# A graph layer's two small matrix products, on halves of the TensorE array and on all of it

## The chip, the cores and the metric

One core of a Trainium2 chip runs the kernel; the other cores are idle. The metric is the device time of one execution in microseconds (us). Two measurements of this kernel agree within about 0.2%.

## The reference

A message-passing layer on 12,500 nodes and 400,000 edges, then a residual and a layer norm. An edge takes the features of its source node, multiplies them with weights that a small network makes of the edge's 64 scalars, and with the edge's four attributes (one scalar `e0`, one vector `e1`); the results are summed by destination node. The edges come sorted by destination. Cut to what matters:

```python
h_s, h_v = (s @ lin1_ws) * a, (v @ lin1_wv) * a          # per node, scaled
hid = silu(edge_scalars @ fc_w1 * _inv(64))               # per edge, 64 wide
w = hid @ fc_w2 * _inv(64)                                # per edge, 224 wide
w1, w2, w3, w4, w5 = split(w, [64, 128, 160, 192])
es, ev = h_s[edge_src], h_v[edge_src]                     # gather
m_s1 = w1 * es * e0
m_s2 = w4 * einsum('eci,ei->ec', ev, e1) * _inv(3)
m_v1 = (w2 * es)[:, :, None] * e1[:, None, :]
m_v2 = w3[:, :, None] * ev * e0[:, :, None]
m_v3 = w5[:, :, None] * cross(ev, e1[:, None, :]) * _inv(2)
agg_s = segment_sum(concat(m_s1, m_s2), edge_dst) / 4
agg_v = segment_sum(concat(m_v1, m_v2, m_v3), edge_dst) / 4
# lin2 on the sums, self-connection, gates, then
x = layernorm(x + concat(silu(scalars), gated))
```

All of it is in fp32.

## The kernel before

**Nodes first.** A stage ahead of the loop computes the node features (`hp`, L283, and `pz`, L298), scales them on DVE and writes them to a table in HBM, `h_tab`.

**Edges in tiles, blocks and steps.** 128 edges are a tile (3125 of them). Three tiles are a block (`BT`), whose edges' destinations lie in a window of 16 nodes (`W`). Blocks go in pairs: an even block is half 0, an odd one half 1. A step of the main loop (L744) handles a quad of four tiles, two of each half; there are 782 steps, the last with one tile. What a step does:

- POOL gathers the source rows, one indirect DMA for each tile, 128 rows of `h_tab` into `hg` (L433). Four `hg` buffers stand in turn, and POOL runs ahead as far as they allow.
- Every second step `hide` makes the hidden layer of two steps ahead: `ph` (L424) multiplies the block-diagonal `w1` (64 + 64 rows) with 128 rows of edge scalars, in which the two halves lie one above the other. ACT applies the silu into `hid` (L426), so the hidden values of half 0 stand in partitions 0 to 63 and those of half 1 in 64 to 127.
- `weights` (L445) makes the 224 weights of each edge: for each tile a product with 64 rows of `hid` as the stationary side and `w2` as the moving side, into one of two `pw` buffers of PSUM. `w2` holds `fc_w2` twice, once for each half of the rows.
- `products` (L455, L463) on DVE multiplies weights and gathered features into `pr`, 416 columns for each tile. `select_quad` (L501, L504) makes the selection on DVE: `oh` says which of the block's 16 nodes an edge goes to, `sel` is that times the four edge attributes, 64 columns for each tile.
- `sum_up`, one step later, adds a tile's edges up on TensorE: `add_tile` (L511) multiplies the tile's `sel` (128 edges by 64) with its `pr` (128 by 416) into `pa`. Half 0 writes the PSUM partitions 0 to 63 and half 1 the partitions 64 to 127, so that a pair of blocks shares one `pa`.
- When both blocks of a pair are summed, ACT copies `pa` to `sa` (L676); two steps later four transposes, `pt` (L520), turn it round. After 16 blocks, `po` (L536) applies the output map: two sums of five 128-row products, one of which has a further one on 32 rows of `t3`, named `po<-t` in the profile. DVE adds the 16 windows into the node sums `acc` at addresses that it reads from `rows` (L544, L720), two in a step.
- Between these, `finish` (L547) closes four tiles of nodes at a time: transposes `pp` (L570) into `z`, gates, residual, moments, norm; and the self-connection `psc` (L656) is added in pieces.

**Order.** The loop's instructions stand on PE, DVE, ACT and POOL in the order of the code (`manual_schedule`). On PE a step is: pw of step n, pp if a job is being turned, the sums of step n-1, ph for step n+2 (every second step), po and pt when due, psc when due. On DVE: the first product, z, reads of window addresses, the other products, `oh`, `sel`, two adds, one step of a closing job. The misc tiles in PSUM (ph, pt, po, pp, psc) share two buffers. SP issues the loads.

**Shapes.** A product on 64 rows, or into 64 columns, uses half of the array, as `128*64` and `64*128` tell in the profile. Every product is fp32 and shows as two weight loads (PEld) and two matmul passes (PE).

After the loop there is a repair path (L807 to L854), which runs only when a block's window is wider than 16 nodes or the schedule's margin is broken. It did not run in this execution.

Of the kernel before, what the change touches and what calls it, by code (L numbers as in the profile page):

```python
# [10 lines left out]
F32 = mybir.dt.float32  # L11
# [9 lines left out]
P = 128  # L21
S = 64
# [6 lines left out]
BT = 3  # L29
EB = BT * P  # L30
W = 16
Q = 4
# [7 lines left out]
NWT = 224  # L40
NPR = 2 * S + 3 * V3
ROWS = 4 * W
# [10 lines left out]
def gnn_kernel(  # L53
# [21 lines left out]
    nc = tc.nc  # L75
# [5 lines left out]
    TT = G * GT  # L81
# [6 lines left out]
    consts = ctx.enter_context(tc.tile_pool(name="consts", bufs=1))  # L88
# [15 lines left out]
    for i in range(2):  # L104
        r = slice(S + i * V, S + (i + 1) * V)
# [126 lines left out]
    w1 = consts.tile([2 * S, 2 * S], F32, name="w1")  # L232
    nc.vector.memset(w1, 0.0)

    w2 = consts.tile([2 * S, NWT], F32, name="w2")
    l2 = consts.tile([P, 11, V3], F32, name="l2")
    nc.vector.memset(l2, 0.0)
    share = ends_pool.tile([1, NB], I32, name="share")
# [6 lines left out]
    with tc.tile_pool(name="nodes", bufs=2) as nodes, tc.tile_pool(  # L245
        name="nodes_ps", bufs=6, space=PSUM
    ) as nps, tc.tile_pool(name="z_ps", bufs=2, space=PSUM) as zps:
        CH = 4 * U * P
        HALF = CH // 2
        for c0 in range(0, N, CH):  # L250
            cn = min(CH, N - c0)
            quarters = 4 if cn == CH else 1
            assert quarters == 4 or cn <= U * P
            xas = []
            for b0 in range(0, cn, HALF):
                bn = min(HALF, cn - b0)
                xa = nodes.tile([P, HALF], F32, name="xa", bufs=3)
                nc.sync.dma_start(xa[:S, :bn], xs_t[:, c0 + b0:c0 + b0 + bn])
                nc.sync.dma_start(xa[S:, :bn], xv_t[:2 * V, c0 + b0:c0 + b0 + bn])
                xas.append(xa)  # L260
            xz = nodes.tile([P, U * P], F32, name="xz")
            cq = cn // quarters
            for q in range(quarters):
                nc.sync.dma_start(xz[q * V:(q + 1) * V, :cq],
                                  xv_t[2 * V:, c0 + q * cq:c0 + (q + 1) * cq])
            if c0 == 2 * CH:
                for half in range(2):
                    r = slice(half * S, (half + 1) * S)
                    nc.sync.dma_start(w1[r, r], fc_w1)
                    at_c = 0  # L270
                    for a, b in ((64, 128), (0, 64), (192, 224), (160, 192), (128, 160)):
                        nc.sync.dma_start(w2[r, at_c:at_c + b - a], fc_w2[:, a:b])
                        at_c += b - a
            ht = nodes.tile([P, 4 * U, D], F32, name="ht")
            nt = -(-cn // P)
            first = c0 // P
            full = cn // P
            for t0 in range(0, nt, U):
                ps = nps.tile([P, U, P], F32, name="hp")
                for t in range(t0, min(t0 + U, nt)):  # L280
                    n = min(P, cn - t * P)
                    e = t * P % HALF
                    nc.tensor.matmul(ps[:n, t - t0], xas[t * P // HALF][:, e:e + n], l1,  # L283
                                     start=True, stop=True)
                k = min(U, full - t0)
                nc.vector.tensor_mul(
                    ht[:, t0:t0 + k, :P], ps[:, :k],
                    at[:, first + t0:first + t0 + k, None].to_broadcast([P, k, P]))
                if t0 + k < nt <= t0 + U:
                    n = cn - full * P  # L290
                    nc.vector.tensor_scalar(ht[:n, full, :P], ps[:n, full - t0],
                                            at[:n, first + full:first + full + 1], None, op0=OP.mult)

            pz = zps.tile([P, U, 4, V], F32, name="pz")
            k = quarters * V
            for u in range(-(-cq // P)):
                n = min(P, cq - u * P)
                nc.tensor.matmul(pz[:n, u, :quarters].rearrange("p q c -> p (q c)"),  # L298
                                 xz[:k, u * P:u * P + n], l1z[:k, :k], start=True, stop=True)
            if quarters == 4:  # L300
                nc.vector.tensor_mul(
                    ht[:, :, P:].rearrange("p (q u) c -> p u q c", q=4), pz,
                    at[:, first:first + 4 * U].rearrange("p (q u) -> p u q", q=4)[:, :, :, None]
                    .to_broadcast([P, U, 4, V]))
            else:
                nc.vector.tensor_mul(ht[:, :full, P:], pz[:, :full, 0],
                                     at[:, first:first + full, None].to_broadcast([P, full, V]))
            if cn > full * P:
                n = cn - full * P
                nc.vector.tensor_scalar(ht[:n, full, P:], pz[:n, full, 0],  # L310
                                        at[:n, first + full:first + full + 1], None, op0=OP.mult)
            nc.scalar.dma_start(
                h_tab[c0:c0 + full * P, :].rearrange("(q p) d -> p q d", p=P), ht[:, :full])
            if cn > full * P:
                nc.scalar.dma_start(h_tab[c0 + full * P:c0 + cn, :], ht[:n, full])
# [99 lines left out]
    def hidden(pool, psum, es, halves, t0, n):  # L415

        ph = psum.tile([2 * S, Q * P], F32, name="ph", tag="misc")
        hid = pool.tile([2 * S, Q * P], F32, name="hid")
        ends = [max(0, min(n, m - t0)) for m in halves]
        assert ends[0] >= ends[1]  # L420
        for k, c0, c1 in ((2 * S, 0, ends[1]), (S, ends[1], ends[0])):
            if c1 > c0:
                c = slice(c0 * P, c1 * P)
                nc.tensor.matmul(ph[:k, c], w1[:k, :k], es[:k, t0 * P + c0 * P:t0 * P + c1 * P],  # L424
                                 start=True, stop=True)
                nc.scalar.activation(hid[:k, c], ph[:k, c], AF.Silu, scale=1.0 / math.sqrt(64))  # L426
        return hid
# [10 lines left out]
    def weights(psum, hid, slots):  # L438

        pw = psum.tile([P, Q, 256], F32, name="pw")  # L440
        n = len(slots)
        for t in sorted(range(n), key=lambda t: (slots[t][1], slots[t][0])):
            half, c = slots[t]
            r = slice(half * S, (half + 1) * S)
            nc.tensor.matmul(pw[:, t, :NWT], hid[r, c * P:(c + 1) * P], w2[r],  # L445
                             start=True, stop=True)
        return pw

# [46 lines left out]
    def select_quad(pool, tiles):  # L495

        n = len(tiles)
        t0 = slot_of[tiles[0][0]]
        u = t0 % AHEAD
        oh = pool.tile([P, Q, W], F32, name="oh4")[:, :n]  # L500
        nc.vector.tensor_tensor(oh, rel[:, t0:t0 + n, None].to_broadcast([P, n, W]),  # L501
                                iota[:, None, :].to_broadcast([P, n, W]), op=OP.is_equal)
        sel = pool.tile([P, Q, 4, W], F32, name="sel")
        nc.vector.tensor_mul(  # L504
            sel[:, :n], oh[:, :, None, :].to_broadcast([P, n, 4, W]),
            by_slot(tiles[0][0])[:, u:u + n, :, None].to_broadcast([P, n, 4, W]))
        return sel

    def add_tile(pa, half, sel, t, pr, start, stop):

        nc.tensor.matmul(pa[half * ROWS:(half + 1) * ROWS, :NPR],  # L511
                         sel[:, t].rearrange("p k w -> p (k w)"), pr, start=start, stop=stop)

    def turned(psum, sa, tt, t3, b, n):

# [98 lines left out]
    with tc.tile_pool(  # L614
# [47 lines left out]
        pas = {}  # L662
# [11 lines left out]
        def close(j, n):  # L674
            sa = late.tile([P, NPR], F32, name="sa")
            nc.scalar.copy(sa, pas.pop(j)[:, :NPR])  # L676
            turns_due.append((n + 2, j, sa))
# [22 lines left out]
        def sum_up(n, tiles, pr, sel):  # L700

            for slot, (t, half, _) in sorted(enumerate(tiles), key=lambda k: (k[1][2], k[1][1])):
                b, m = divmod(t, BT)
                j = b // 2
                assert b % 2 == half
                if j not in pas and m == 0:
                    pas[j] = pa_ps.tile([P, 512], F32, name="pa")
                stop = m == BT - 1 or t == TT - 1
                add_tile(pas[j], half, sel, slot, pr[:, slot], start=(m == 0), stop=stop)
                if stop:  # L710
                    ended.add(b)
                    if {2 * j, 2 * j + 1} <= ended:
                        close(j, n)

        def add_up(n):

# [91 lines left out]
        with tc.For_i(0, n_redo, 1):  # L808
# [5 lines left out]
            with tc.For_i(0, n_again, 1) as g, tc.For_i(0, GT, 1) as k:  # L814
# [21 lines left out]
                with tc.For_i(first + W, last + 1, W) as base:  # L836
# [1 line left out]
                        base, 0, N - 1, skip_runtime_bounds_check_because="it is at most `last`")  # L838
                    pa = pa_ps.tile([P, 512], F32, name="pa")
                    sel = select(late, r, eat)  # L840
                    add_tile(pa, 0, sel, 0, pr[:, 0], start=True, stop=True)
                    sa = late.tile([P, NPR], F32, name="sa")
                    nc.scalar.copy(sa[:ROWS], pa[:ROWS, :NPR])
                    tt = late.tile([P, 7, NO, W], F32, name="tt", bufs=1)
# [56 lines left out]
```

## Time and profile before

| What | Value |
|---|---|
| Time, median of 10 runs | 4089.33 us (4087.28 to 4093.45) |
| The profiled execution: time | 4091.91 us |
| The profiled execution: span | 4090.0 us |
| Mean granted TensorE clock | 0.929 |
| Start of the first pw, second sum, last sum | 92.21, 134.34, 4055.78 us |
| HBM traffic, mean | 100 GB/s |

The profile gives an instruction's line, engine, operation and the tiles that it writes and reads (`pa<-pr,sel`), its partitions and elements, its count, busy time and mean duration, and the idle time of its engine ahead of it with what ended it. For PE, `128*64 128x416` is a stationary side of 128 rows and 64 columns, and 416 columns that stream through it. "Busy" is the union of an engine's instructions in time, so overlapping passes count once. The granted clock is the share of full speed that TensorE was given; in this profile it is either 1 or one half at any moment.

### The profile page before, as it was taken

Reading aid. Unit: us, or ns where it says so; the run is one execution under the profiler, and the core shown is the slowest. Engines: PE = TensorE matmul, PEld = TensorE weight load, DVE = VectorE, ACT = ScalarE, POOL = GpSimd, SP = SyncE. Lnnn points to the kernel's source line nnn. Section 1 sums busy time; section 2 is a strip of 40 time slices with the busy share of each in tenths; the row PEclk is TensorE's granted clock in tenths of the full one; section 3 lists DMA queues with packets and bytes.
Section 4 is the critical chain, followed back from the end, with each engine's and each line's share of the span. In section 5 each row is a group of like instructions: output and inputs, shape, how many; then the busy total and the mean of one; then the engine's idle time right before and its main releaser. Section 6 shows DMA issues by size and latency. Waiting matters only on the chain.

```text
span 4090.0 us, 56919 instructions
## 1 busy us (share of the span) xinstructions
PE 3312.5 (81%) x17386; PEld 1601.3 (39%) x17386; DVE 2527.5 (62%) x6359; ACT 932.2 (23%) x3007; POOL 3010.8 (74%) x3134
## 2 busy tenths in 40 slices
PE   4678888888887888887888888788888788788886
PEld 4334433433443443343343343343334334334333
DVE  2665665666666666666656666666666666666665
ACT  0111221222222222222222122122222222222221
POOL 3677777777777777777777777777777777777774
PEclk7899999999999998999999999999999999999998
DMA  7434443443443443434434334344343443443431
GB/s 207 109 92 100 102 104 95 101 101 97 101 101 98 104 98 98 108 94 101 102 97 106 95 100 106 94 101 102 98 109 90 100 110 90 104 105 90 105 93 48
DMA packets 292610, 414.51 MB, mean 101 GB/s; under 512 B 74869, under 2 KB 239618, under 8 KB 292053
## 3 DMA queue, kind: packets, MB, share of 16 engines
q0 software_dynamic: 150000, 256.20, 24.1%
q1 hardware_dynamic: 128770, 145.95, 15.6%
q10 hardware_dynamic: 13526, 8.64, 0.7%
q8 instruction: 141, 2.31, 0.2%
q14 instruction: 173, 1.41, 0.1%
HBM read 394.54 MB, written 16.01 MB: 100 GB/s over the span
## 4 chain that ended last, share of the span: by engine, by line
POOL 28%; issue 22%; DMA 19%; DVE 14%; PE 13%; DVEq 3%; ACTq 0%; ACT 0%; POOLq 0%; SPq 0%
POOL hg L433 28%; DMA hg<-h_tab,idx 18%; DVE pr L463 8%; PE pa L511 5%; DVE pr L455 2%; PE ph L424 2%; PE pw L445 2%; DVEq L720 2%; PE po L536 2%; DVE acc L544 1%; PE pt L520 1%; DVE sel L504 1%; DVE oh L501 1%; DMA h_tab<-ht 1%; PE hp L283 0%
## 5 line engine op out<-in xcount | busy, mean ns | idle before, releaser
L433 POOL DMA_INDIRECT hg<-h_tab,idx x3125 | 2988.1, 956 | 1036.9 <-issue 905.7
L511 PE MATMUL pa<-pr,sel 128*64 128x416 f32 x6250 | 1372.0, 562 | 631.3 <-DVE acc L544 324.4
L455 DVE TENSOR_TENSOR pr<-pw,hg 128x512 f32<-128x512 f32 x782 | 540.3, 691 | 1325.5 <-DMA hg<-h_tab,idx 1011.6
L463 DVE TENSOR_TENSOR pr<-pw,hg 128x384 f32<-128x384 f32 x2346 | 1205.6, 552 | 90.2 <-issue 22.4
L511 PEld LDWEIGHTS pa<-pr,sel 128*64 128x64 f32 x6250 | 411.2, 143 | 1212.0 <-issue 746.7
L445 PE MATMUL pw<-w,hid 64*128 64x224 f32 x6250 | 821.9, 377 | 17.1 <-ACT hid L426 17.1
L445 PEld LDWEIGHTS pw<-w,hid 64*128 64x128 f32 x6250 | 544.0, 187 | 319.5 <-issue 301.1
L676 ACT COPY sa<-pa 128x416 f32<-128x416 f32 x521 | 263.1, 505 | 1170.7 <-PE pa L511 1170.5
L424 PE MATMUL ph<-es,w 128*128 128x512 f32 (+1 forms) x784 | 490.2, 710 | 1.9 <-DMA es<-in_es_t_dram 1.3
L426 ACT ACTIVATE hid<-ph 128x512 f32<-128x512 f32 x392 | 233.5, 596 | 973.7 <-PE ph L424 973.2
L520 PEld LDWEIGHTS pt<-ident,sa 128*128 128x128 f32 (+1 forms) x2084 | 225.7, 135 | 343.1 <-issue 235.6
L504 DVE TENSOR_TENSOR sel<-oh,eas 128x256 f32<-128x256 f32 x782 | 333.6, 427 | 37.1
L520 PE MATMUL pt<-ident,sa 128*128 128x128 f32 (+1 forms) x2084 | 336.4, 285 | 4.9 <-DVE z L571 4.9
L536 PE MATMUL po<-tt,l 128*96 128x256 f32 (+3 forms) x1340 | 317.3, 384 | 3.1 <-ACT t L527 3.1
L524 ACT COPY tt<-pt 128x192 f32<-128x192 f32 x521 | 164.8, 316 | 475.5 <-PE pt L520 471.4
L536 PEld LDWEIGHTS po<-tt,l 128*96 128x96 f32 x1340 | 206.6, 164 | 126.3 <-issue 64.4
L424 PEld LDWEIGHTS ph<-es,w 128*128 128x128 f32 x784 | 130.9, 210 | 303.9 <-issue 277.9
L544 DVE TENSOR_TENSOR acc<-acc,os 96x32 f32 x1042 | 194.3, 186 | 30.2 <-DVE acc L544 8.9
L501 DVE TENSOR_TENSOR oh<-rel,iota 128x64 f32<-128x64 int16 x782 | 174.7, 223 | 0.0
L539 ACT COPY os<-po 96x512 f32<-96x512 f32 (+2 forms) x67 | 38.2, 570 | 314.8 <-PE po L536 296.4
L526 ACT COPY tt<-pt 128x32 f32<-128x32 f32 x521 | 102.9, 198 | 0.0
L426 ACT ACT_TABLE_LOAD x47 | 60.3, 1283 | 173.6 <-PE ph L424 91.3
(70 smaller groups left out, 748.9 us busy)
## 6 DMA issues: line engine op xcount, KB each, us to landing
es<-in_es_t_dram SPq DMA_DIRECT2D x260, 384.0 KB
hg<-h_tab,idx POOLq DMA_INDIRECT x3125
h_tab<-ht ACTq DMA_DIRECT2D x6, 1280.0 KB
xt<-in_x_dram SPq DMA_DIRECT2D x23, 320.0 KB
out_dram<-y SPq DMA_DIRECT2D x23, 320.0 KB
xv<-in_xv_t_dram SPq DMA_DIRECT2D x25, 187.5 KB
eat<-in_ea_dram SPq DMA_DIRECT2D x30, 120.0 KB
xs<-in_xs_t_dram SPq DMA_DIRECT2D x25, 125.0 KB
```

The source lines that it names most:

```text
L424: nc.tensor.matmul(ph[:k, c], w1[:k, :k], es[:k, t0 * P + c0 * P:t0 * P + c1 * P], start=True, stop=True)
L426: nc.scalar.activation(hid[:k, c], ph[:k, c], AF.Silu, scale=1.0 / math.sqrt(64))
L433: nc.gpsimd.indirect_dma_start(out=hg[:, t, :], out_offset=None, in_=h_tab, in_offset=bass.IndirectOffsetOnAxis(ap=i, axis=0))
L445: nc.tensor.matmul(pw[:, t, :NWT], hid[r, c * P:(c + 1) * P], w2[r], start=True, stop=True)
L455: nc.vector.tensor_mul(two, pw[:, :n, :2 * S].rearrange("p t (k c) -> p t k c", k=2), hg[:, :n, None, :S].to_broadcast([P, n, 2, S]))
L463: nc.vector.tensor_mul(pr[:, :n, first:first + V3].rearrange("p t (i c) -> p t i c", i=3), pw[:, :n, None, 2 * S + k * V:2 * S + (k + 1) * ...
L504: nc.vector.tensor_mul(sel[:, :n], oh[:, :, None, :].to_broadcast([P, n, 4, W]), by_slot(tiles[0][0])[:, u:u + n, :, None].to_broadcast([P ...
L511: nc.tensor.matmul(pa[half * ROWS:(half + 1) * ROWS, :NPR], sel[:, t].rearrange("p k w -> p (k w)"), pr, start=start, stop=stop)
L520: nc.tensor.transpose(pt[:c, four * P:four * P + k], sa[:k, four * P:four * P + c], ident[:k, :k])
L536: nc.tensor.matmul(po[:, k, :nb], l2[:b, terms[to, part, four]], a[:, :nb], start=(n == 0), stop=(n == len(of) - 1))
L544: nc.vector.tensor_add(window, window, os[:, :, b])
L676: nc.scalar.copy(sa, pas.pop(j)[:, :NPR])
```

## The change

**Weights.** `w2` becomes two maps, one for each half: rows 0 to 63 of map 0 and rows 64 to 127 of map 1 hold `fc_w2`, the other rows are zero. The product takes all 128 rows of `hid`, both halves' hidden values, and the zero rows take the wrong half out.

**Sums.** The selection has 128 columns for each tile, 64 for half 0 and 64 for half 1; the columns of the other half are zero. They are zeroed once, in two buffers that the steps use in turn. The selection's multiplication on DVE is done for each half. The product then writes all 128 partitions of `pa`, and a pair's six products are one accumulation, begun by the first tile of half 0 and ended by whichever tile comes last.

The number of products is the same: 3125 for the weights and 3125 for the sums.

```diff
-    w2 = consts.tile([2 * S, NWT], F32, name="w2")
+    w2 = consts.tile([2 * S, 2, NWT], F32, name="w2")
+    nc.vector.memset(w2, 0.0)
...
-                        nc.sync.dma_start(w2[r, at_c:at_c + b - a], fc_w2[:, a:b])
+                        nc.sync.dma_start(w2[r, half, at_c:at_c + b - a], fc_w2[:, a:b])
...
+                if k < 2 * S:
+                    nc.vector.memset(hid[k:, c], 0.0)
...
-            r = slice(half * S, (half + 1) * S)
-            nc.tensor.matmul(pw[:, t, :NWT], hid[r, c * P:(c + 1) * P], w2[r],
+            nc.tensor.matmul(pw[:, t, :NWT], hid[:, c * P:(c + 1) * P], w2[:, half],
                              start=True, stop=True)
...
-        sel = pool.tile([P, Q, 4, W], F32, name="sel")
-        nc.vector.tensor_mul(
-            sel[:, :n], oh[:, :, None, :].to_broadcast([P, n, 4, W]),
-            by_slot(tiles[0][0])[:, u:u + n, :, None].to_broadcast([P, n, 4, W]))
+        sel = sels[t0 // Q % len(sels)]
+        eas = by_slot(tiles[0][0])
+        for half in range(2):
+            k = slice(2 * half, min(2 * half + 2, n))
+            m = k.stop - k.start
+            if m > 0:
+                assert all(h == half for _, h, _ in tiles[k])
+                nc.vector.tensor_mul(
+                    sel[:, k, half], oh[:, k, None, :].to_broadcast([P, m, 4, W]),
+                    eas[:, u + k.start:u + k.stop, :, None].to_broadcast([P, m, 4, W]))
...
-    def add_tile(pa, half, sel, t, pr, start, stop):
-
-        nc.tensor.matmul(pa[half * ROWS:(half + 1) * ROWS, :NPR],
-                         sel[:, t].rearrange("p k w -> p (k w)"), pr, start=start, stop=stop)
+    sels = [consts.tile([P, Q, 2, 4, W], F32, name=f"sel{k}") for k in range(2)]
+    for sel in sels:
+        nc.vector.memset(sel, 0.0)
+
+    def add_tile(pa, sel, t, pr, start, stop):
+
+        nc.tensor.matmul(pa[:, :NPR], sel[:, t].rearrange("p h k w -> p (h k w)"), pr,
+                         start=start, stop=stop)
...
-                stop = m == BT - 1 or t == TT - 1
-                add_tile(pas[j], half, sel, slot, pr[:, slot], start=(m == 0), stop=stop)
+                if m == BT - 1 or t == TT - 1:
+                    ended.add(b)
+                stop = {2 * j, 2 * j + 1} <= ended
+                add_tile(pas[j], sel, slot, pr[:, slot], start=(m == 0 and half == 0), stop=stop)
                 if stop:
-                    ended.add(b)
-                    if {2 * j, 2 * j + 1} <= ended:
-                        close(j, n)
+                    close(j, n)
```

The repair path's one product keeps 64 columns and is written out there in place of `add_tile`.

More of the change, by code (lines that the diff above doesn't have):

```diff
@@ L840, in gnn_kernel @@
                     sel = select(late, r, eat)
-                    add_tile(pa, 0, sel, 0, pr[:, 0], start=True, stop=True)
+                    nc.tensor.matmul(pa[:ROWS, :NPR], sel[:, 0].rearrange("p k w -> p (k w)"),
+                                     pr[:, 0], start=True, stop=True)
                     sa = late.tile([P, NPR], F32, name="sa")
```

## The prediction, made before the changed kernel was run

> **What bounds the kernel now.** First the page, its busy shares and costliest groups.
>
> ```profile
> PE 3312.5 (81%) x17386; PEld 1601.3 (39%) x17386; DVE 2527.5 (62%) x6359; ACT 932.2 (23%) x3007; POOL 3010.8 (74%) x3134
> ...
> L433 POOL DMA_INDIRECT hg<-h_tab,idx x3125 | 2988.1, 956 | 1036.9 <-issue 905.7
> L511 PE MATMUL pa<-pr,sel 128*64 128x416 f32 x6250 | 1372.0, 562 | 631.3 <-DVE acc L544 324.4
> ...
> L445 PE MATMUL pw<-w,hid 64*128 64x224 f32 x6250 | 821.9, 377 | 17.1 <-ACT hid L426 17.1
> ```
>
> PE is busiest by share, but POOL's 74% leave out the 0.30 us that it needs between two gathers. So I read one window of the loop (columns: length; busy us and instructions of PE, PEld, DVE, ACT, POOL; clock; DMA):
>
> ```profile
> 2000.00:3000.00 1000.00, 827.92 (x4348) 395.59 (x4347) 630.95 (x1590) 238.87 (x768) 758.44 (x794) 0.94 0.40 100
> ```
>
> POOL issues 794 gathers in 1000 us, one per 1.26 us, which is 0.95 busy plus 0.30 between. It never rests: 4 gathers, one step of the loop, take 5.04 us, and 3125 take some 3935 of the 4090 us. PE has slack. The timeline of PE shows how its work is packed (start, length, line, shapes, count, idle before):
>
> ```profile
> 2195.16 1.13 PE L424 MATMUL ph<-es,w 128*128 128x512 f32 x2
> 2196.12 0.60 PE L520 MATMUL pt<-ident,sa 128*128 128x128 f32 x4
> 2196.65 1.03 PE L445 MATMUL pw<-w,hid 64*128 64x224 f32 x8
> 2197.61 1.62 PE L511 MATMUL pa<-pr,sel 128*64 128x416 f32 x8
> 2199.15 0.66 PE L520 MATMUL pt<-ident,sa 128*128 128x128 f32 x4
> ...
> 2212.25 3.04 PE L511 MATMUL pa<-pr,sel 128*64 128x416 f32 x8 [3.65 <-DVE sel L504]
> ```
>
> Every fp32 product is two passes, so a step's four products are x8. The last row took 3.04 us instead of 1.62 after an idle stretch of 3.65 us: the granted clock had halved there. Narrow windows give the cost of one pass:
>
> ```profile
> 2195.69 0.59 PE L424 MATMUL ph<-es,w 128*128 128x512 f32 x1
> ```
> ```profile
> 2181.07 0.87 PE L511 MATMUL pa<-pr,sel 128*64 128x416 f32 x4
> ```
> ```profile
> 2184.15 0.55 PE L445 MATMUL pw<-w,hid 64*128 64x224 f32 x4
> ```
>
> The second ph pass starts at 2195.69 and its successor at 2196.12: 512 columns stream in 0.43 us, 0.84 ns a column (the rest of 0.59 is pipeline, overlapped). In the pa row four passes are two pairs: 0.87 less one pass's median of 0.513 is 0.36 us from pair to pair, of which 0.007 is the offset inside a pair. So a pair costs 0.349, just 416 columns by 0.84: its two passes, one per column group, stream at the same time. Likewise 0.55 less 0.35 leaves 0.19 per pair of pw, 224 columns by 0.84. The half-array shapes now get two passes for the price of one.
>
> **The change part by part.** Weights and sums. Both shapes become 128*128, so passes no longer pair. A step's sums go from 4 x 0.349 = 1.40 us to 8 x 0.349 = 2.79, its weights from 0.76 to 8 x 0.189 = 1.51: +2.14 us of streaming a step, 1672 us in 781 steps. POOL's slack does not cover that, so I add up what PE must stream in the loop: pa 6250 x 0.349 = 2181; pw 6250 x 0.189 = 1181; ph 782 x 0.428 = 335; pt 2084 x 0.109 = 227 (four in 0.44 us); po 64 full groups x 5.1 (10 + 2 + 10 passes, from 2186.83 to 2192.09 on the timeline, less 0.17 for entering) + 8 for the short ones = 334; pp 196 x 0.11 = 21; psc 100 x 0.42 = 42. Sum 4321 us, 5.53 a step against POOL's 5.04: PE becomes the bound.
>
> Switches of shape. In the rows above ph to pt, both full array, takes 0.43, streaming alone; but pt to pw takes 0.53 for four passes of 0.109, so 0.09 extra, and pw to pa 0.96 for 0.76, so 0.2 (the wait for the array to empty and the first load, which isn't hidden then). After the change pw, pa, ph, pt and pp all have the full array; the switch remains around the two po<-t passes (within the 5.1). There are 782 pw, 782 pa, 391 ph, 521 pt, 98 pp and 50 psc groups: 2624. At nothing each they add 0; at 0.18 each 472 us. I take nothing, by the ph-to-pt row and by the stage before the loop, where full-array groups follow each other:
>
> ```profile
> 52.05 0.50 PE L283 MATMUL hp<-l,xa 128*128 128x128 f32 x3
> ```
> ```profile
> L283 PEld LDWEIGHTS hp<-l,xa x196: 153/193/334, 7.2 to 71.8; 128*128 128x128 f32 x194, 128*84 128x84 f32 x2
> L283 PE MATMUL hp<-l,xa x196: 272/276/582, 7.2 to 72.0; 128*128 128x128 f32 x194, 128*84 128x128 f32 x2
> ```
>
> Three passes end 0.50 after the first start; less 0.276 that is 0.112 a pass, though each has its own 128-column load of 0.193. So full-array loads run under the passes before them. The new pw pass (0.189) and pa pass (0.349) are longer than this and hide the same load. A drained pt, whose last load fills 32 columns only, may still cost 0.09 before pw: 468 x 0.09 = 42 us, kept for the range.
>
> This is where a rule speaks against the change: the Trainium skill, "TensorE: Matmul & The Clock Gate", Part 3 under "What overlaps and what doesn't", says that a weight load overlaps a running matmul only when it goes to other rows of the array. With all 128 rows in every pass, 12500 loads of pw and pa would then stand in the open; at the 0.19 us of this trace's rows that would be about 2375 us more, some 6860 in all. The hp rows (0.112 a pass with a load of 0.193) contradict it, and I go by them.
>
> DVE. The selection is written as two 128x128 products instead of one of 128x256 (0.427 us). No row has 128x128 with these operands; the bounds are nothing extra and a whole second one (+0.43), and between the 128x64 oh (0.223) and 128x256 the line gives 0.29, so +0.155 a step, 121 us of DVE work. DVE is idle 38% and its chain from pw to sel is this:
>
> ```profile
> 2218.06 0.69 DVE L455 TENSOR_TENSOR pr<-pw,hg 128x512 f32<-128x512 f32 x1
> 2218.77 1.72 DVE L463 TENSOR_TENSOR pr<-pw,hg 128x384 f32<-128x384 f32 x3
> 2220.40 0.27 DVE L501 TENSOR_TENSOR oh<-rel,iota 128x64 f32<-128x64 int16 x1
> 2220.71 0.42 DVE L504 TENSOR_TENSOR sel<-oh,eas 128x256 f32<-128x256 f32 x1
> ```
>
> That is 3.07 us, with the split 3.22, with the z of a closing job (0.41) 3.63, plus some 0.4 to hand over from PE and back: 3.6 to 4.0. Between the end of pw(n) and sum(n), PE now has at least sum(n-1) and pw(n+1), 2.79 + 1.51 = 4.30, and 5.53 on average. So the work of DVE hides; if it didn't, +0.155 in each of 781 steps is the 121 us. Adds (0.41) and moments or norm (up to 1.4) come behind sel and run into the 4.30; I allow 10 us for the few steps where they push the next sel past it.
>
> The rest. Three more memsets on DVE (w2 448, two selections of 512 elements; by the 0.94 us for 1056 about 1.3 us) stand ahead of its first eviction, where it is idle 6.89 us. The ten loads of w2 on SP stay ten. Scaling w2 over 448 columns costs some 0.2 us once, the memset of hid's lower rows runs once in the last chunk, and the changed product in the repair loop does not run. The sums' waits are the old ones, on DVE for pr and sel; the second product now also needs the second half of sel. Behind that wait stand ph, po, pt and the next pw, which is counted above. Two selection buffers as before: DVE writes one only after the sum of two steps ago, which PE did before the pw that DVE itself needed. POOL, no longer the bound, waits for hg buffers, four deep, and what it lost there costs nothing.
>
> The end. In the trace the loop really starts with the second sum at 134.34; of the 4321 PE has by then done three pw, two ph and one sum, 9 us. The clock there is half until about 140, which adds 3. From the last sum (4055.78) to the end of the span are 34 us, with 7 of PE's 4321 in them. So 134 + 4312 + 3 - 7 + 34 + 10 = 4486 us of span; the profiled run took 4091.91 for a span of 4090.0, so 4488, and it lies 2.6 above the median of 4089.33. I say 4487.
>
> **The rivals.** (1) Switches still cost 0.18 although all is full array, because the groups begin with semaphore waits: 4487 + 472 = 4960. For it: nearly all switches in the loop now cost this. Against: ph to pt, with a wait, is at 0.43.
> (2) PE cannot keep its feed: DVE's chain is past 4.30 in many steps, and idle stretches bring the half clock back. The loop's clock is 0.94 now; PE's 4312 at 0.94 would take 275 more, 4760; sums late by 0.5 us in a third of the steps cost 130, 4620. Against: before, idle stretches of PE come from gathers that DVE waits for (1011.6 us in the waits), and these will be ahead.
> (3) Not slower: records of pairs only look concurrent, the ends of matmuls being modelled, and a full-array pass costs what one record's share does now, 0.175 and 0.095. Then PE stays under POOL, and saved switches may even shorten the waits: 4070 to 4090. It decides from where a pa pass and a pw pass together are under (5.04 - 1.23) / 8 = 0.476 us, 1.23 being the other groups' (4321 - 3362) / 781; the rows give 0.538. Against: ph, alone on the array, streams at exactly the same 0.84 ns a column.
>
> **How the numbers follow.** Forecast 75%, (1) 8%, (2) 14%, (3) 3%. The forecast's own range is 4450 to 4560: below, no allowance (10) and the rounding of a pass (0.002 us on 12500 passes is 25); above, the 42 of pt and 30 of late sums. With the nearer half of (2) the range is 4435 to 4650. Two measurements of this kernel differ by 0.15%; within 0.2% counts as the same. Faster 1%, same 2%, slower 97%.
>
> **What would show it.** PE at 97% or more, clock at 0.99 in the loop, passes of pa 0.349 apart and of pw 0.189, pw to pa without the 0.09 (right); POOL with waits for buffers and only 0.67 busy; DVE's wait in front of L455 turned from the gather to pw. Wrong, if PE's idle before the sums stays at hundreds of us (2), if gaps of 0.1 to 0.2 stand between groups (1), or POOL still issues every 1.26 us (3).

## The result and the profile after

The changed kernel takes 4499.54 us (median of 8 runs, 4497.62 to 4501.99), the kernel before 4090.53 us in the same comparison (28 runs): 1.1 times, interval 1.0991 to 1.101. The forecast was 4487, with a range of 4435 to 4650. The profiled execution has a span of 4499.8 us. Its busy shares and the groups that answer to those shown before:

```profile
PE 4387.4 (98%) x17386; PEld 3010.5 (67%) x17386; DVE 2583.8 (57%) x7144; ACT 931.4 (21%) x3007; POOL 3003.1 (67%) x3134
...
L437 POOL DMA_INDIRECT hg<-h_tab,idx x3125 | 2980.5, 954 | 1441.1 <-issue 810.8
L525 PE MATMUL pa<-pr,sel 128*128 128x416 f32 x6250 | 2316.1, 513 | 28.5 <-DVE sel L513 28.5
...
L458 DVE TENSOR_TENSOR pr<-pw,hg 128x512 f32<-128x512 f32 x782 | 540.5, 691 | 1615.6 <-PE pw L448 1548.4
L448 PE MATMUL pw<-w,hid 128*128 128x224 f32 x6250 | 1316.0, 353 | 15.8 <-ACT hid L430 15.8
...
L513 DVE TENSOR_TENSOR sel<-oh,eas 128x128 f32<-128x128 f32 x1563 | 391.1, 291 | 37.5 <-DVE oh L504 0.5
```

PE waited 631 us ahead of the sums before and waits 28.5 now, 25.6 of it in the first step. The wait has moved to DVE. Before, DVE stood for the gathers:

```profile
L455 DVE TENSOR_TENSOR pr<-pw,hg 128x512 f32<-128x512 f32 x782 | 540.3, 691 | 1325.5 <-DMA hg<-h_tab,idx 1011.6
```

Now it stands for `pw` (1548 us). A pass of the sums still lasts 0.513 us (the median before, the mean after), and the weight loads are as many as before (17386); what grew is the time that the passes take together, since no two of them stream side by side any more. One window of the loop:

```profile
2000.00:3000.00 1000.00, 998.50 (x3937) 682.57 (x3937) 586.25 (x1632) 216.88 (x693) 685.78 (x720) 1.00 0.37 91
```

PE is busy 998.5 us of 1000 and the clock is full (0.94 before). POOL issues 720 gathers in place of 794. The chain of work that ended last, in which POOL led before, is now nearly PE alone (first line before, the others after):

```profile
POOL 28%; issue 22%; DMA 19%; DVE 14%; PE 13%; DVEq 3%; ACTq 0%; ACT 0%; POOLq 0%; SPq 0%
...
PE 96%; DMA 2%; DVE 1%; ACT 0%; issue 0%; DVEq 0%; SPq 0%; ACTq 0%
PE pa L525 48%; PE pw L448 26%; PE ph L428 7%; PE po L550 7%; PE pt L534 5%; PE psc L670 1%; DMA h_tab<-ht 1%; DMA xa<-in_xv_t_dram 1%; PE pp L584 0%; PE hp L285 0%; ACT hid L430 0%; DMA xa<-in_xs_t_dram 0%; DMA dt<-in_dst_dram 0%; DVEq L734 0%; DVE rel L390 0%
```

And PE's own timeline shows how closely the groups now stand:

```profile
2018.58 1.02 PE L428 MATMUL ph<-es,w 128*128 128x512 f32 x2
2019.44 0.60 PE L534 MATMUL pt<-ident,sa 128*128 128x128 f32 x4
2019.88 1.68 PE L448 MATMUL pw<-w,hid 128*128 128x224 f32 x8
2021.39 2.96 PE L525 MATMUL pa<-pr,sel 128*128 128x416 f32 x8
2024.18 0.60 PE L534 MATMUL pt<-ident,sa 128*128 128x128 f32 x4
```

From start to start: ph 0.86, pt 0.44 (0.53 before), pw 1.51 (0.96 before), pa 2.79 (1.54 before). These are 2, 4, 8 and 8 passes of 0.43, 0.109, 0.189 and 0.349 us with nothing between them (a transpose, as in pt, is one pass, any other product two).

### The profile page after: what moved, and what is told of

It is laid out like the page before. It is cut to its first block, busy times and chain, and to the rows that moved or that the text cites. A ratio compares the mean times of both kernels' runs of the same rounds, so it can differ in the third digit from the quotient of the medians.

```text
span 4499.8 us, 57596 instructions
## 1 busy us (share of the span) xinstructions
PE 4387.4 (98%) x17386; PEld 3010.5 (67%) x17386; DVE 2583.8 (57%) x7144; ACT 931.4 (21%) x3007; POOL 3003.1 (67%) x3134
## 4 chain that ended last, share of the span: by engine, by line
PE 96%; DMA 2%; DVE 1%; ACT 0%; issue 0%; DVEq 0%; SPq 0%; ACTq 0%
PE pa L525 48%; PE pw L448 26%; PE ph L428 7%; PE po L550 7%; PE pt L534 5%; PE psc L670 1%; DMA h_tab<-ht 1%; DMA xa<-in_xv_t_dram 1%; PE pp L584 0%; PE hp L285 0%; ACT hid L430 0%; DMA xa<-in_xs_t_dram 0%; DMA dt<-in_dst_dram 0%; DVEq L734 0%; DVE rel L390 0%
## 5 line engine op out<-in xcount | busy, mean ns | idle before, releaser
L525 PE MATMUL pa<-pr,sel 128*128 128x416 f32 x6250 | 2316.1, 513 | 28.5 <-DVE sel L513 28.5
L525 PEld LDWEIGHTS pa<-pr,sel 128*128 128x128 f32 x6250 | 1180.5, 190 | 776.8 <-issue 745.7
L448 PE MATMUL pw<-w,hid 128*128 128x224 f32 x6250 | 1316.0, 353 | 15.8 <-ACT hid L430 15.8
L448 PEld LDWEIGHTS pw<-w,hid 128*128 128x128 f32 x6250 | 1146.4, 190 | 144.5 <-issue 88.8
L513 DVE TENSOR_TENSOR sel<-oh,eas 128x128 f32<-128x128 f32 x1563 | 391.1, 291 | 37.5 <-DVE oh L504 0.5
L428 PE MATMUL ph<-es,w 128*128 128x512 f32 (+1 forms) x784 | 401.4, 594 | 3.0 <-DMA es<-in_es_t_dram 2.5
L534 PEld LDWEIGHTS pt<-ident,sa 128*128 128x128 f32 (+1 forms) x2084 | 237.5, 130 | 231.8 <-issue 221.4
L534 PE MATMUL pt<-ident,sa 128*128 128x128 f32 (+1 forms) x2084 | 312.7, 273 | 0.0
L428 PEld LDWEIGHTS ph<-es,w 128*128 128x128 f32 x784 | 149.5, 191 | 127.8 <-issue 126.1
```

What stands on the lines that cost most here:

```text
L448: nc.tensor.matmul(pw[:, t, :NWT], hid[:, c * P:(c + 1) * P], w2[:, half], start=True, stop=True)
L513: nc.vector.tensor_mul(sel[:, k, half], oh[:, k, None, :].to_broadcast([P, m, 4, W]), eas[:, u + k.start:u + k.stop, :, None].to_broadcast ...
L525: nc.tensor.matmul(pa[:, :NPR], sel[:, t].rearrange("p h k w -> p (h k w)"), pr, start=start, stop=stop)
L534: nc.tensor.transpose(pt[:c, four * P:four * P + k], sa[:k, four * P:four * P + c], ident[:k, :k])
```

## The experiments

Each was run beside the kernel before on the same chip; times are medians.

**One part alone (e1, e2).** e1 is the kernel before with this of the change:

```diff
-            nc.tensor.matmul(pw[:, t, :NWT], hid[r, c * P:(c + 1) * P], w2[r],
+            nc.tensor.matmul(pw[:, t, :NWT], hid[:, c * P:(c + 1) * P], w2[:, half],
```

(and the two maps with zeros); e2 has the 128-column selection and the sums into all of `pa`, and the weights as before.

> The kernel before with the weights alone on the whole array; the sums stay on 64 columns. Theory (the loop runs at the slower of POOL's gathers, 5.04 us a step, and the sum of PE's passes, in which a full-array pass costs as much as a pair did, plus 0.1 to 0.2 us where the array's shape changes): PE needs 4321 - 1091 = 3230 us of streaming and some 270 for entering and leaving the sums' shape, 4.5 us a step, less than POOL's 5.04, so the time stays at 4075 to 4105. Rival (each part adds its own share, the 409 us split by streaming 590 to 1091): 4234. A second rival (all of the added streaming shows): 4680.

Measured: 4095.51 us beside 4094.97, ratio 1.0002 (0.9992 to 1.0012). The same window of its loop:

```profile
2000.00:3000.00 1000.00, 925.15 (x4369) 547.81 (x4367) 631.35 (x1594) 242.45 (x773) 757.99 (x795) 0.97 0.43 100
```

PE took on 97 us of busy time in 1000 (925 in place of 828), and POOL still issues a gather every 1.26 us: the step is still POOL's, and what the weights cost is hidden behind it.

> The kernel before with the sums alone on the whole array; the weights stay on 64 rows. Theory: PE needs 4321 - 590 = 3731 us and 0.4 a step for entering and leaving the weights' shape, 4044, which is 5.18 us a step, just over POOL's 5.04; with the 179 us outside: 4220, between 4150 and 4260, with POOL nearly back to back too. If the changes of shape cost nothing: 4090. Rival (shares by streaming): 4356. Rival (all of the sums' added streaming shows): 5180.

Measured: 4207.16 us beside 4094.97, ratio 1.0273 (1.0256 to 1.029), 13 us under the estimate of 4220. PE is busy 998.1 of 1000 us in the same window and POOL issues 772 gathers. Its timeline on PE:

```profile
2010.47 3.06 PE L523 MATMUL pa<-pr,sel 128*128 128x416 f32 x8
2013.37 1.02 PE L425 MATMUL ph<-es,w 128*128 128x512 f32 x2
2014.23 0.60 PE L532 MATMUL pt<-ident,sa 128*128 128x128 f32 x4
2014.76 1.03 PE L446 MATMUL pw<-w,hid 64*128 64x224 f32 x8
2015.72 0.62 PE L523 MATMUL pa<-pr,sel 128*128 128x416 f32 x1
```

ph to pt is 0.86, as in the changed kernel. Around the half-row pw the groups take longer than their streaming: pt 0.53 for 0.44, pw 0.96 for 0.76, and the full-array pa behind it 2.90 for 2.79, together 0.40 us a step. So a change of the array's shape costs here, and a change of line or buffer does not. Putting the weights on the whole array as well (the changed kernel) adds 4499.5 - 4207.2 = 292 us, though their streaming grows by 6250 x 0.189 / 2 = 590. The missing 298 us are 0.38 for each of 782 steps: what entering and leaving the half shape had cost.

**Half of the gathers (e3, e4).** In both kernels:

```diff
-        for t, i in enumerate(idx):
+        for t, i in enumerate(idx[:2]):
             nc.gpsimd.indirect_dma_start(
...
```

with four `hg` tiles that stay in place and are zeroed once.

> The kernel before, in which only the first two of a step's four tiles are gathered; the other two are read as zeros, so the products of half of the edges are zero. Theory (POOL's gathers set the time before the change): POOL needs 2.5 us a step, and the time falls to what PE and DVE need: PE 2640 us of streaming and some 470 for changes of shape, with 179 outside 3290; with waits between PE and DVE 3300 to 3550. Rival (PE already sets the time, by its 81%): above 3950.

> The changed kernel with the same two of four gathers, the other two tiles read as zeros. Theory (PE's passes alone set the time): 4490 to 4500, no change, though POOL's work is halved. Rival (gathers or DMA still hold up the changed kernel in places): 4400 or less.

Measured: e3 3344.88 us (0.8168 of the kernel before, 0.8155 to 0.8182), e4 4500.79 us. Halving the gathers takes 750 us from the one and nothing from the other. (It halves POOL's instructions and their transfers alike; the two are not told apart here.) Behind the gathers lay a PE that needs 3.3 ms with halves and 4.5 with the whole array: without that bound the change would have cost 1156 us, and the gathers hid 750 of these. e3's busy shares:

```profile
PE 3128.1 (94%) x17386; PEld 1546.4 (46%) x17386; DVE 2499.3 (75%) x6359; ACT 929.0 (28%) x3007; POOL 1625.9 (49%) x1576
```

**The order within a step (e5).** The kernel before, its half-array products sorted by half:

```diff
-        for t in sorted(range(n), key=lambda t: (slots[t][1], slots[t][0])):
+        for t in sorted(range(n), key=lambda t: (slots[t][0], slots[t][1])):
```

and likewise for the sums.

> The kernel before, with the same half-array products in another order: a step's two tiles of half 0 first, then the two of half 1, for the weights and for the sums. Theory (two passes stream at once only where passes of different halves stand next to each other in PE's order): a run of four passes of one half, then four of the other, of which one pair overlaps at most, 7 times 0.349 and 7 times 0.189, 3.77 us a step in place of 2.15; PE then needs 2941 + 959 + 525 for changes of shape, 4425 us in the loop, and the time is 4450 to 4620, about the changed kernel's without any whole-array product. Rival (the array pairs passes of the two halves whatever their order within the step): 4075 to 4105, no change.

Measured: 4085.85 us beside 4085.15, ratio 0.9998 (0.9988 to 1.0008). The theory fell and the rival holds. Its timeline on PE, a step's sums and a narrow window over their first pair:

```profile
2000.36 1.62 PE L511 MATMUL pa<-pr,sel 128*64 128x416 f32 x8
2001.92 1.13 PE L424 MATMUL ph<-es,w 128*128 128x512 f32 x2
```
```profile
2000.36 0.58 PE L511 MATMUL pa<-pr,sel 128*64 128x416 f32 x2
```

Eight passes still take 1.62 us. In the narrow window two passes that both run in it take 0.58 us from the first start to the last end, hardly more than one first pass (0.513, and 0.05 for its load, which nothing hides); so the second starts some 0.01 us after the first. In the rows before, one pair follows the other after some 0.35 us, so the second pass is read as one of the other half (the records do not name the half), though the four passes of the first half all stand ahead of it in the program. The pairs do not come from neighbours in the order; each half's passes go ahead on their own part of the array, at least over the eight of one step.

**PE made shorter again (e6).** The changed kernel with

```diff
-                add_tile(pas[j], sel, slot, pr[:, slot], start=(m == 0 and half == 0), stop=stop)
+                if m != 1 or stop:
+                    add_tile(pas[j], sel, slot, pr[:, slot], start=(m == 0 and half == 0), stop=stop)
```

> The changed kernel without the sum of each block's middle tile, whose edges are left out; gathers, weights and products are all still made. Theory (slower of PE's passes and POOL's gathers): PE loses 1041 products of 2 x 0.349, 727 us, and falls to 4.6 us a step, so POOL's 5.04 set the time again: 4075 to 4110. Rival (PE's passes alone set the time at all sizes): 4500 - 727 = 3773.

Measured: 4075.46 us beside 4085.15, ratio 0.9974 (0.9963 to 0.9985). With PE at an estimated 4.6 us a step the time is POOL's again:

```profile
2000.00:3000.00 1000.00, 946.86 (x3829) 658.57 (x3828) 643.68 (x1801) 239.81 (x764) 757.82 (x796) 0.98 0.43 101
```

There are 796 gathers in 1000 us, with whole-array shapes throughout. Of 727 us of passes taken away only 424 show; then POOL's floor is reached.

**What the weights cost unhidden (e7, and once more in e8 to e11).** e1's kernel with e3's two gathers:

> The weights alone on the whole array, as in e1, with the two of four gathers of e3 and e4 (the other two tiles read as zeros), so that POOL no longer hides anything. Theory (a part that was free in e1 was free only behind the gathers): against e3's 3344.9, 6250 passes that no longer pair add 590 us, and some 780 changes of shape that fall away (into pw from ph, pt and po, and from pw to pp) give 0.2 each back, 155: 3780, between 3720 and 3840. Rival (the changes of shape saved pay for the weights, so that the part is free by itself): 3345.

Measured: 3679.1 us, under the expected range of 3720 to 3840. So the part is not free by itself, but costs 334 us against e3 where 435 were expected. PE's waits in e3 say where most of the missing 101 us went (engine, line, what it waited for: us, times, longest):

```profile
PE pa L517 <- DVE acc L550: 55.6, 63, 2.0
PE pa L517 <- DVE sel L510: 55.0, 65, 26.1
...
PE pp L576 <- DVE acc L550: 17.6, 26, 2.7
```

With halves and half of the gathers, PE waits 128 us for DVE; in e7 the same three waits come to 36. The longer weights give DVE time, and 92 of the 101 us are that. In e7's comparison the kernel before took 5271 us at a granted clock of 0.83, on a chip that no other experiment was on; in the other comparisons it took 4085 to 4095. Four kernels were therefore run together on one more chip:

> The kernel before itself, for a trace on the chip that the next three run on. In e7 it took 5271 us at a granted clock of 0.83, and 4085 to 4095 in the other comparisons. Theory (POOL's gathers set its time, and on that chip they came more slowly): where its time is above 4150, the time from one gather to the next is longer than 1.26 us in the same measure, and passes of PE have their old length; 4085 to 4095 on a chip like the others.

> The changed kernel on the same chip. Theory: 4495 to 4505 wherever POOL's gathers take less than PE's 5.53 us a step, that is below 1.38 us each; on a chip with slower gathers the time of the kernel before, since the gathers set both.

> The kernel of e3 on the same chip: 3335 to 3355, whatever the gathers do.

> The kernel of e7 on the same chip: 3670 to 3690. Of the 780 us of changes of shape and pairs that were expected against e3 before (435 more), 93 are waits of PE for DVE in e3 (128 us, against 36 in e7), which the longer weights cover; so 330 to 345 more than e10.

(The expected gain of e7 was 435 us; the last expectation means that number.) Measured: 4083.35, 4500.34, 3344.96 and 3678.25 us, beside 4085.43. So unhidden, the weights cost 333 us and the sums the other 822 of 1155. This split depends on the order: with the sums first (e2, where PE is busy throughout) they cost 862 us over e3 and the weights 292 more. e7's number stands on both chips. What held the kernel before up on that one chip was not seen. No trace of it was taken there, and the theory of slower gathers, which e8 was to show, was not put to the test, since the next chip was like the others; e7, with half of the gathers, ran at its usual time there, and its gathers lasted 1.027 us beside 1.024 in e3.

The 1156 us are less than the 1672 us of streaming that the change adds by the prediction's sum. PE's waits for DVE ahead of the sums and of pp fall from 128 us in e3 to 32 in the changed kernel. The other 420 us, 0.54 a step, are left for the changes of shape that fall away, and the rows before have about this much over pure streaming: 0.09 in pt, 0.20 in pw, 0.15 in pa (1.54 for 1.40) and 0.10 in the ph behind it (0.96 for 0.86).

## Why the prediction was right

**The bound and its price.** A pass of the whole array was predicted at a pair's cost, 0.349 and 0.189 us, and the timeline after has these. 6250 x 0.538 = 3362 us of the 4321 were therefore right. That PE takes the place of POOL is shown from both sides: with POOL's work halved nothing changes (e4), with PE's cut to under 5.04 us POOL is back (e6).

**Changes of shape at nothing.** They were taken at 0 with 472 us as the other bound. pt to pw is 0.44 for four passes after the change, so even the pt that fills only 32 columns last costs nothing; the 42 us kept for it fall away. Rival (1), 4960, is out. For psc alone the 0 did not hold (see below). The loads run under the passes, as the hp rows had it: in the groups shown pw passes start 0.189 us apart although each has a load of 0.190. The rule of the Trainium skill that the prediction weighed ("TensorE: Matmul & The Clock Gate", Part 3, "What overlaps and what doesn't"), a load beside a running matmul only on other rows, does not hold for these loads; by it the time would have been near 6860.

**DVE's feed.** Half of the split selection was put between 0.223 and 0.427 us, at 0.29; it is 0.291. PE's wait for it is 2.9 us after the first step, so the 10 us allowed for late sums were not needed, and rival (2), at 4620 to 4760, is out: clock 1.00 in the loop, where 0.94 was its premise.

**Rival (3)** took the records of pairs as not really concurrent, so that a whole-array pass would cost 0.175 and 0.095 us. The rows after have 0.349 and 0.189 from pass to pass, so it is out.

**Where the 13 us are.** The span is 4499.8, the sum made 4486. From the second sum to the start of the last the trace has 135.12 to 4466.00, 4330.9 us; the sum had 4312 + 3 - 7 + 10 = 4318 there. The term that was too small is psc, put at 0.42 us a pass with nothing for its change of shape. The prediction counted its 50 groups among those whose change costs nothing, but psc is 64*96 or 96*96 and not the full array. Two places on PE:

```profile
1996.31 0.60 PE L534 MATMUL pt<-ident,sa 128*128 128x128 f32 x4
1996.84 1.08 PE L670 MATMUL psc<-xs,scs 64*96 64x500 f32 x2
1997.85 1.40 PE L448 MATMUL pw<-w,hid 128*128 128x224 f32 x6
...
2003.11 0.60 PE L534 MATMUL pt<-ident,sa 128*128 128x128 f32 x4
2003.96 1.08 PE L670 MATMUL psc<-xv,scv 96*96 96x500 f32 x2 [0.25 <-ACT hid L430]
2004.88 1.68 PE L448 MATMUL pw<-w,hid 128*128 128x224 f32 x8
```

From pt to pw, less pt's 0.44, is 1.10 us with the 64-row psc and 1.33 with the other, which waits for ACT to free the shared PSUM buffer. Against 0.84 that is 0.26 and 0.49, 25 times each, 19 us. This, less the 10 us that late sums did not need, leaves 9 of the 13; the second sum's start, 0.8 us later, and the rounding of passes are of the size of the rest. So the forecast came this close partly by luck: one term was 19 us too small and another 10 us too large.

## What to carry to other kernels

Two half-array products on different halves of the array cost one pass for the two here, and padding with zeros gives this up; it gives back some 0.2 us wherever the array had to change shape, so count both before choosing. A part that costs nothing behind another engine (the weights in e1) has its price, here 292 us, as soon as the next part lifts its engine over that floor: add up each engine's work per step and compare the sums, not the busy shares. To see what lies behind a bound, halve the bound's work in both kernels.

## What was not expected of the hardware

The two halves' passes ran side by side even where all of a half's products stood before the other's in the program (e5, starts some 0.01 us apart). And more work did not lower the granted clock here: it was 0.94 in the loop before at 83% busy PE, 0.97 at 93% (e1) and 1.00 at 99.8%. The half clock goes with PE's waits, as in the row before with 3.65 us of idle time and passes at half speed behind it.
